# Eighty-eight fixed elementwise operations become the scheduler's choice between VectorE and GpSimd, with changed cost formulas and a newly searched schedule

## The chip, the cores and the metric

The kernel runs as one program on one core of a Trainium2 chip. The metric is the device time of one execution in microseconds (us); before and after are compared as medians of several executions. A profile is one further execution, recorded by the hardware. Its engines are called PE (TensorE's matmuls), PEld (TensorE's weight loads), DVE (VectorE), ACT (ScalarE), POOL (GpSimd) and SP (SyncE, which issues transfers).

## The reference

A four-layer decoder over x (8 batches of 256 tokens, 256 features) with a context of 77 tokens per batch. Each layer is an attention, a cross attention and a feed-forward part, each with a residual sum and a layer norm after it; most parts are of another kind in every layer. Two parts matter here. The cross attention of layer 2 normalises its queries per head (16 features) and rotates pairs of them:

```
q = _layernorm(q, qn_w, qn_b)
qp = q.reshape(b, h, s, d // 2, 2)
qe, qo = (qp[..., 0], qp[..., 1])
out = jnp.stack([qe * cos - qo * sin, qe * sin + qo * cos], axis=-1)
```

Layer 3 begins with a state-space block, whose output is gated, and goes on with a linear cross attention, whose queries and keys pass a softmax over the 16 features of each head:

```
y = _rmsnorm(y * jax.nn.silu(z), norm_w)
...
q = jax.nn.softmax(_heads(x @ Wq.T + bq), axis=-1)
k = jax.nn.softmax(_heads(y @ Wk.T + bk), axis=-1)
```

The other parts (quantised attention in layer 0, mixtures of experts, attention with learned features, a butterfly feed-forward) are computed as before.

## The kernel before

Tokens are in 16 tiles of 128; a batch is two tiles, a block four. Nearly all matrix products are float32, with tiles of 128x128 (or 32, 64 or 77 rows or columns for heads), accumulating in eight PSUM banks. Every layer runs its parts batch by batch, and generators interleave parts that don't depend on each other: in layer 3 the state-space block of one batch (`inputs`, `weights`, `outputs`) runs beside the cross attention (`cross`) and the feed-forward part (`dense`) of earlier ones.

The order in which each engine works is not the program's own. The class `Arrange` builds the program once, turns it into a graph of some 20,900 instructions and schedules it by a list scheduler, engine by engine, with a cost in ns for each instruction (`cost`: how long it holds its engine, and when its result is there), for matmuls that follow each other (`pair`), for signals between engines (`SIGNAL`) and for two states of TensorE's clock. The program is then built again with that order tied in (`chain`). A stretch of 100 instructions is scheduled with one of eight pairs of slack factors; the string `CHOICE` has one digit per stretch, found by a search outside of the kernel. So each change of a cost or a digit can move instructions anywhere behind it.

Some operations may run on either of two engines: `either` records both forms, and the scheduler takes the one that it can start first. Before the change these are copies from PSUM (`copy`, L612 on DVE and L613 on ACT), copies with a bias or a scale (L619, L620, L626), the first tap of the convolution (L2655 or L2656) and the differences in `weights` of layer 3 (L2697 or L2700).

The operations that the change frees are, with their fixed engines before:

- L2 cross attention, `rotated`, per batch: two strided products u (L2304, POOL), q times own (L2308, DVE), plus more (L2309, DVE), and their sum into qpad (L2310, POOL). The result is transposed by PE (L779). The rotation of batch b+2 is issued while batch b is weighed.
- L3 `outputs`, the gate: after each pair of L2747 (DVE) one product y times zs (L2752, POOL); ACT squares it (L2756), POOL sums the squares (L2757), and PE adds them over partitions.
- L3 `head_softmax`, for queries (q, 128x512) and for keys (kv, 77x256): maximum (L2933), subtraction (L2934, DVE), exponential (L2935, ACT), sum and reciprocal (L2937, L2938, DVE), and the division as a product (L2939, POOL). PE takes kv as weights (L633) and transposes q (L2801).

Lines that the text also speaks of: the norms are bn_stats (L730), POOL's scale and power for the inverse root (L660, L661) and the application (L741; in layer 3, in place, L2782), which PE transposes next (L713; L2843). POOL's sums of x and a row are L753, L2796 and L2854. L2661 are the other taps of the convolution, L2863 the Gelu of `dense`. L1713 belongs to the routing of layer 0's experts, and L2246 are memsets that prepare layer 2's cross attention.

## Time and profile before

| what | value |
|---|---|
| median of three runs | 3106.22 us (3105.67 to 3116.44) |
| the profiled execution | 3120.3 us, span 3118.6 us |
| mean granted TensorE clock | 0.944 |
| PE, DVE, ACT, POOL busy | 2951.5, 1666.5, 1217.5, 932.5 us |
| PE busy in the first 468 us | 395.9 us |
| PE busy from 2184 to 2418 us (L2 cross attention) | 219.3 us |
| PE busy from 2652 to 3120 us (most of L3) | 422.5 us |
| activation table loads on ACT | 58, 1.283 us each |

The page gives busy time per engine, then the span in 40 slices of 78 us: each digit is the busy share in tenths, and PEclk the granted clock in tenths of full speed. A row of the windows view gives a stretch, its length, then busy us and the number of instructions of PE, PEld, DVE, ACT and POOL, then the granted clock, the share of transfers and GB/s. A row of the waits view gives who waited, for whom, us in total, how often, and the longest. The view of one line gives its instructions with minimum, median and maximum duration in ns; the timeline gives start, duration, engine and line.

### The profile page before, as it was taken

The page shows a single profiled execution, that of the slowest core. Times are in us where ns is not written, and L with a number is a line of the kernel's source. Part 1 is how long each engine was busy: PE and PEld are TensorE (multiplying, and loading weights), DVE is VectorE, ACT ScalarE, POOL GpSimd, SP SyncE. Part 2 cuts the span into 40 slices and gives each one's busy share as a digit, 9 for nine tenths or more (in the row PEclk, how much of TensorE's full clock was granted, in tenths as well). Part 3 has the DMA queues.
Part 4 walks back from the last instruction along what each step waited for, and adds up shares of the span by engine and source line. Part 5 has one row for each costly group of instructions (what it writes and reads, how often), then busy time and mean ns, then how long its engine had stood idle before and what let it go on. Part 6 is the DMA issues. An engine that isn't in the chain of part 4 may idle for free. (4 is left out here: it accounts for less than half of the span.)

```text
span 3118.6 us, 49555 instructions
## 1 busy us (share of the span) xinstructions
PE 2951.5 (95%) x19200; PEld 2162.8 (69%) x19200; DVE 1666.5 (53%) x4467; ACT 1217.5 (39%) x2725; POOL 932.5 (30%) x1413
## 2 busy tenths in 40 slices
PE   6899979989998999999999999999899999999997
PEld 4456557768886777776555777566577687677876
DVE  7878776660003666775112221366677542678872
ACT  4667544433332334443111111255344233355442
POOL 2222353353323221332000000322244463535342
PEclk7879879999998999999999999999888999989998
DMA  5424550125542000011010243300000564100000
GB/s 188 137 94 160 202 193 27 33 88 201 195 175 97 18 8 10 28 61 54 11 56 1 97 145 122 98 28 8 1 15 32 186 242 157 32 11 4 8 8 11
DMA packets 136364, 252.87 MB, mean 81 GB/s; under 512 B 14962, under 2 KB 104826, under 8 KB 128442
## 3 DMA queue, kind: packets, MB, share of 16 engines
q1 hardware_dynamic: 112298, 150.80, 14.5%
q0 software_dynamic: 22672, 97.77, 9.0%
q8 instruction: 155, 2.54, 0.3%
q10 hardware_dynamic: 1152, 1.05, 0.1%
q14 instruction: 87, 0.71, 0.1%
HBM read 162.32 MB, written 87.26 MB: 80 GB/s over the span
## 5 line engine op out<-in xcount | busy, mean ns | idle before, releaser
L633 PE MATMUL ps<-xt,w 128*128 128x256 f32 (+1 forms) x1408 | 443.6, 462 | 4.9 <-issue 4.3
L633 PE MATMUL ps<-w,hT 128*128 128x256 f32 (+1 forms) x1704 | 378.7, 379 | 0.0
L633 PEld LDWEIGHTS ps<-xt,w 128*128 128x128 f32 x1408 | 260.8, 192 | 148.0 <-issue 124.3
L633 PEld LDWEIGHTS ps<-w,hT 128*128 128x128 f32 (+1 forms) x1704 | 313.2, 186 | 53.5 <-issue 5.2
L633 PE MATMUL ps<-gT,w 128*128 128x256 f32 (+2 forms) x1472 | 337.1, 386 | 1.0 <-ACT gT L613 0.7
L633 PEld LDWEIGHTS ps<-gT,w 128*128 128x128 f32 x1472 | 263.1, 190 | 67.7 <-ACT hT L1662 2.9
L633 PE MATMUL ps<-w,oT 128*128 128x256 f32 x704 | 162.0, 382 | 0.0
L753 POOL TENSOR_TENSOR xb<-x,rows 128x256 f32<-128x256 f32 x80 | 59.2, 743 | 301.6 <-DVE res L758 294.5
L633 PEld LDWEIGHTS ps<-w,oT 128*128 128x128 f32 x704 | 131.7, 190 | 22.3 <-issue 2.5
L613 ACT COPY y<-ps 128x512 f32<-128x512 f32 (+2 forms) x65 | 31.0, 476 | 251.9 <-PE ps L633 243.2
L1735 ACT ACTIVATE hT<-ps 128x512 f32<-128x512 f32 x56 | 33.4, 597 | 233.7 <-PE ps L633 233.7
L1160 ACT ACTIVATE e<-ps,nm 128x128 bf16<-128x128 f32 (+1 forms) x256 | 103.5, 441 | 38.3 <-DVE nm L1155 30.9
L1739 DVE TENSOR_TENSOR hT<-hT,ps 128x512 f32<-128x512 f32 x56 | 38.5, 687 | 146.7 <-PE ps L633 146.5
L612 DVE COPY gT<-ps 128x256 f32<-128x256 f32 (+1 forms) x12 | 4.6, 391 | 209.1 <-PE ps L1607 170.8
L613 ACT COPY oT<-ps 128x256 f32<-128x256 f32 (+1 forms) x130 | 58.2, 448 | 112.6 <-PE ps L1882 55.5
L2093 DVE SCALAR_TENSOR_TENSOR f<-ps,f 128x512 f32<-128x512 f32 x128 | 79.2, 682 | 30.3 <-ACT f L2092 30.2
L1984 DVE TENSOR_TENSOR hT<-hT,ps 128x320 f32<-128x320 f32 x64 | 31.2, 487 | 117.2 <-PE ps L633 117.2
L1662 ACT ACTIVATE hT<-ps,more 128x256 f32<-128x256 f32 (+1 forms) x152 | 70.1, 462 | 55.8 <-PE ps L633 55.3
L613 ACT COPY xt<-ps 128x256 f32<-128x256 f32 (+2 forms) x105 | 44.3, 432 | 116.8 <-PE ps L713 92.1
L2092 ACT ACTIVATE f<-ps,neg 128x512 f32<-128x512 f32 x128 | 77.5, 693 | 30.2 <-PE ps L2089 30.1
L1400 ACT ACTIVATE P<-P 128x616 f32<-128x616 f32 (+1 forms) x48 | 42.6, 888 | 115.3 <-DVE P L1439 114.9
L661 POOL TENSOR_TENSOR rs<-rs,mhalf 128x1 f32<-128x1 f32 x144 | 80.5, 563 | 9.4
(675 smaller groups left out, 6507.8 us busy)
## 6 DMA issues: line engine op xcount, KB each, us to landing
l2x<-zero SPq DMA_DIRECT2D x28, 1024.0 KB
l0x<-zero SPq DMA_DIRECT2D x16, 1024.0 KB
w<-in_L_ffn_rg SPq DMA_DIRECT2D x8, 1024.0 KB
w<-in_L_ffn_ru SPq DMA_DIRECT2D x8, 1024.0 KB
w<-in_L_ffn_rd SPq DMA_DIRECT2D x8, 1024.0 KB
l0e<-y SPq DMA_DIRECT2D x17, 256.0 KB
l2e<-y SPq DMA_DIRECT2D x15, 256.0 KB
rows<-in_rows SPq DMA_DIRECT2D x7, 544.0 KB
```

Source lines behind the costliest of these rows:

```text
L613: ("Activation", ("InstTensorCopy", None), lambda: nc.scalar.copy(out, in_)),
L633: self.nc.tensor.matmul(out, lhsT, rhs, start=(i == 0), stop=(i == last))
L661: self.nc.gpsimd.tensor_tensor(out, out, self.mhalf[: in_.shape[0], :w], ALU.pow)
L753: self.nc.gpsimd.tensor_tensor(t, self.X[i], row, ALU.add)
L1160: nc.scalar.activation(e[:, : (t + 1) * P], ps[j][:, i, :], AF.Exp, bias=nm[:, t, h : h + 1], accum_out=z[:, t, h : h + 1],)
L1400: nc.scalar.activation(pr, pr, AF.Exp, scale=0.125)
L1662: nc.scalar.activation(hT[:, f + m, :w], ps[:, m * 256 : m * 256 + w], func, bias=more[:, f + m : f + m + 1])
L1735: nc.scalar.activation(hT[:, f, :], ps, func, **({"bias": bias(f)} if bias else {}))
L1739: nc.vector.tensor_tensor(hT[:, f, :], hT[:, f, :], ps, ALU.mult)
L1984: nc.vector.tensor_tensor(hT[:, f, :CAP], hT[:, f, :CAP], ps[:, :CAP], ALU.mult)
L2092: nc.scalar.activation(f[:, j], ps[j], AF.Exp, bias=neg1)
L2093: nc.vector.scalar_tensor_tensor(f[:, j], ps[j], 1.0, f[:, j], ALU.max, ALU.min)
```

## The change

A helper `product` makes an operation of two SBUF tiles free between DVE and POOL, and the operations above go through it. At the same time five formulas in `cost` change: float32 matmuls, DVE operations with a pointer scalar and two SBUF tiles, ACT's copies, ACT's activations with an accumulated sum, and ACT's activations of 500 to 600 elements. The string `CHOICE` is another one (209 digits, of which 53 differ, the first of them the sixth). So the order changes on every engine from layer 0 on.

```diff
-            own = n / 2.4 * (1 if not wide or turn else 4) + 3
+            own = n / 2.4 * (1 if not wide or turn else 4) + (9 if wide and not turn else 3)
...
             s = 65 + n / 0.96
+            pairs = sum(self.count(x.ap) > 200 for x in ins) > 1
             if n <= 256 and ps and kind == "InstTensorScalarPtr" or kind == "InstCopyPredicated":
                 s += 60
+            elif kind == "InstTensorScalarPtr" and pairs and not ps:
+                s += 72
...
             if kind == "InstTensorCopy":
-                s = 23 + 0.9 * n
-                return s, s + 115
-            s = 144 + 0.83 * n + (108 if last else 0) + (45 if not ps and 64 < n <= 512 else 0)
+                s = 118 + 0.746 * n
+                return s, s + 110
+            s = 144 + 0.83 * n + ((87 if n < 200 else 46) if last else 0) + (45 if not ps and 64 < n <= 512 else 0)
+            if 500 < n < 600:
+                s -= 50
...
+    def product(self, out, a, b, op=ALU.mult):
+        nc = self.nc
+        self.either(*(
+            (w, ("InstTensorTensor", None), lambda e=e: e.tensor_tensor(out, a, b, op))
+            for w, e in (("DVE", nc.vector), ("Pool", nc.gpsimd))
+        ))
+
...
                 for u in range(2):
-                    nc.gpsimd.tensor_tensor(
-                        u2[:, :, :, u::2], q[:, :, :, 1 - u :: 2], over(other[:, :, :, u]), ALU.mult
-                    )
+                    self.product(u2[:, :, :, u::2], q[:, :, :, 1 - u :: 2], over(other[:, :, :, u]))
                 flat = lambda t: t.rearrange("p t d u -> p t (d u)")
-                nc.vector.tensor_tensor(u1, q, over(flat(own)), ALU.mult)
-                nc.vector.tensor_tensor(u1, u1, over(flat(more)), ALU.add)
-                nc.gpsimd.tensor_tensor(qp, u1, u2, ALU.add)
+                self.product(u1, q, over(flat(own)))
+                self.product(u1, u1, over(flat(more)), ALU.add)
+                self.product(qp, u1, u2, ALU.add)
...
-                        nc.gpsimd.tensor_tensor(y[:, h, :], y[:, h, :], zs[:, h, :], ALU.mult)
+                        self.product(y[:, h, :], y[:, h, :], zs[:, h, :])
...
-        nc.vector.tensor_tensor(q, q, bc(m), ALU.subtract)
+        self.product(q, q, bc(m), ALU.subtract)
...
-        nc.gpsimd.tensor_tensor(q, q, bc(z), ALU.mult)
+        self.product(q, q, bc(z))
```

More of the change, by code (lines that the diff above doesn't have):

```diff
@@ L78 @@
     PART, TRIALS = 100, ((1.0, 1.0), (0.5, 0.5), (2.0, 2.0), (2.0, 0.5), (0.5, 2.0), (0.25, 0.25), (4.0, 1.0), (1.0, 4.0))
-    CHOICE = "21111100022110201121001101001100121011210222022111000101101010101012110000000022022202222222222222211111001010010100010000000010010110100110100201010100221121012111111101111000120011111011000121111010011010111"
+    CHOICE = "21111002120111001121021011220111111111011102122111000101101010101010112000000001022212222122222222211101001010010101010000000010111010100110121201010110220001010121111111111000100010100111111101011010010011111"
     def __init__(self, g):
```

## The prediction

> **What bounds the kernel now.** First the page: the busy row, the slices and the granted clock.

> ```profile
> PE 2951.5 (95%) x19200; PEld 2162.8 (69%) x19200; DVE 1666.5 (53%) x4467; ACT 1217.5 (39%) x2725; POOL 932.5 (30%) x1413
> ...
> PE   6899979989998999999999999999899999999997
> ...
> PEclk7879879999998999999999999999888999989998
> ```

> TensorE is busy 95% of the span of 3118.6 us: only some 167 us are open, and they lie at the two ends (slices 1 to 6 and 29 to 40). The clock falls in the same places. Its mean is 0.944. Cut into windows, the trace shows stretches at 0.50 (2228.5 to 2252 us) and at 1.00, so about 2 x 0.056 x 3118.6 = 349 us run at half speed. That costs up to half of them, 175 us: as much as the idle time. Then the windows in which the rescheduled products lie, L2's cross attention (the first row) and L3 (the others), with columns PE, PEld, DVE, ACT, POOL, clock:

> ```profile
> 2262.00:2340.00 78.00, 76.57 (x708) 54.67 (x706) 60.42 (x216) 33.74 (x76) 32.24 (x45) 0.89 0.04 15
> 2808.00:2886.00 78.00, 70.30 (x415) 57.45 (x414) 63.78 (x152) 44.27 (x80) 38.14 (x53) 0.96 0.01 4
> 2886.00:2964.00 78.00, 74.89 (x445) 63.87 (x444) 63.80 (x160) 38.31 (x70) 30.98 (x49) 1.00 0.02 8
> 3042.00:3120.00 78.00, 57.55 (x253) 47.39 (x251) 22.45 (x68) 16.92 (x33) 14.62 (x32) 0.86 0.03 11
> ```

> DVE is the fullest helper there (64 of 78 us), GpSimd has room. Last TensorE's own waits, from 2652 to 3042 and (last line) from 3042 us on:

> ```profile
> PE ps L2843 <- DVE x L2782: 5.8, 5, 1.8
> ...
> PE ps L633 <- POOL kv L2939: 2.9, 1, 2.9
> ...
> PE ps L633 <- POOL zs L2757: 0.8, 1, 0.8
> PE ps L2801 <- POOL q L2939: 0.6, 1, 0.6
> ```
> ```profile
> PE ps L2843 <- DVE x L2782: 7.6, 3, 3.8
> ```

> So the products themselves end few waits. What TensorE waits for most is the normalisation x of L2782, on DVE.

> **The change part by part.** Durations of the moved products (minimum/median/maximum ns, by line):

> ```profile
> L2752 POOL TENSOR_TENSOR w<-w,zs x16: 1262/1270/1319, 2772.6 to 3033.7; 128x512 f32<-128x512 f32 x16
> ```
> ```profile
> L2939 POOL TENSOR_TENSOR kv<-kv,hv x8: 616/630/1108, 2663.7 to 2739.3; 77x256 f32<-77x256 f32 x8
> L2939 POOL TENSOR_TENSOR q<-q,hv x8: 1057/1062/2591, 2810.1 to 3064.9; 128x512 f32<-128x512 f32 x8
> ```
> ```profile
> L2934 DVE TENSOR_TENSOR kv<-kv,hm x8: 357/414/541, 2660.3 to 2736.3; 77x256 f32<-77x256 f32 x8
> L2934 DVE TENSOR_TENSOR q<-q,hm x8: 684/1078/1436, 2807.0 to 3061.1; 128x512 f32<-128x512 f32 x8
> ```

> *Where they go.* The order of the changed program puts on DVE 14 of the 16 gate products (L2752), all 8 q and all 8 kv divisions (L2939), and on GpSimd one q and one kv subtraction (L2934). In L3 GpSimd loses 14 x 1.27 + 8 x 1.06 + 8 x 0.63 = 31.3 us and gains, at its own division rows, 1.06 + 0.63: 29.6 us less. DVE gains 22 x 0.69 + 8 x 0.41 - 1.1 = 17.4 us. The planner also moves five copies (0.43 us) and nine of L2655/L2697 (0.48 us) off DVE to ScalarE: 6.5 us. Net +11 us on DVE. In L2's rotation 5 of 16 u products and 2 of 8 last sums go to DVE, 3 of 8 q-own products and 6 of 8 sums to GpSimd: at 0.84 and 1.27 us on GpSimd, 0.42 (the 128x256 rows) and 0.69 on DVE, that is 2.7 us off DVE and some 4 us onto GpSimd. Both are hidden: the rotation of batch b+2 runs while batch b is weighed, and GpSimd is busy 32 of 78 us. Uncovered they would cost those 4 us.

> *What gets shorter.* (a) The 2.9 us wait for kv: its reciprocal ended at 2662.31, but GpSimd was at a power, a copy and a memset and began the product at 2663.70. On DVE, where the reciprocal stands, it would end near 2662.8 instead of 2664.35: -1.5 us; behind that the matmuls wait for nothing else in the row. (b) q ready earlier: -0.6. (c) The gate pair 2 x (1.27 - 0.69) = 1.2 earlier: -0.8 for zs. (d) L2782 is held by GpSimd:

> ```profile
> 3032.43 2.54 POOL L2752 TENSOR_TENSOR w<-w,zs 128x512 f32<-128x512 f32 x2
> ...
> 3032.70 1.14 DVE L2782 TENSOR_SCALAR x<-x,mv,rs 128x256 f32<-128x256 f32 x1
> ```

> It takes 1.14 us instead of 0.41 and ends 0.15 us behind the first product; TensorE then waits 1.01 us for it. In the changed order 16 matmul records stand between the two transposes that wait here: -1.0. At 3064.44 the second x is held likewise by a q division; now that division (0.69) stands ahead of it on DVE instead: -0.2. (e) The first rotation (TensorE waits 0.8 us for qpad): its u pair took 2.60 us on GpSimd; now each engine takes one: -0.8. Sum of (a) to (e): -4.9 us.

> *What is added.* No wait on another engine: the products now follow their makers on DVE. Behind them queue the norms (bn_stats, L2782). ACT gets five more table loads in L2's shared part and L3, 5 x 1.283 = 6.4 us (58 to 63 in all), chiefly Gelu, exp and Gelu again within a batch. ACT is under 60% busy there, so TensorE's work on the next batch hides it. Bounds of both: 0 if all is hidden, 11 + 6.4 = 17.4 if all lands on the path. I take +2, nearest to the rows that show room.

> *What is only reordered.* TensorE's tile shape changes go from 965 to 946 (39 fewer ahead of L2's expert block, 20 more behind it). A 128x256 float32 matmul starts 0.216 us after its like and 0.309 us where the next shape is 77*64: 0.093 x 19 = -1.8. In L2's two attentions six copies leave DVE (2.6 us) with the 2.7 above, beside a DVE busy 171 of 234 us at a reduced clock: I take -2, of 0 to -5.3. The new search touches L0 most, where orders move farthest. No row prices that: its bounds are the 72 us that TensorE idles in the first 468 us on one side and as much added on the other; the rows nearest to it are the three runs of one order, which spread by 10.8 us. Are the corrected costs nearer to the trace? float32 128x256 pairs start 432 ns apart (the planner said 430, now 436), ScalarE's 128x512 activations 476 (569, now 519), DVE's two-tile L2661 396 (332, now 404), but ScalarE's 128x256 copies about 268 at the tightest (253, now 309). Mostly yes: -3.

> *The sum.* -4.9 + 2 - 1.8 - 2 - 3 = -9.7, say -10 us. The profiled execution took 3120.3 us (span 3118.6, 1.7 around it), so by its rows 3110. It is 14 us above the median of 3106.2; carried over, the forecast is **3096 us** (-0.3%).

> *A rule to weigh.* The rows show DVE held until a GpSimd operation ends, also in two-input products: q's L2934 takes up to 1.436 us against 0.684. [...]

> **The rivals.**
> 1. *The clock decides (faster).* If the shorter stalls spare a tenth of the 175 us lost at half speed, the time is 3106 - 10 - 17 = 3079. For it: the low-clock stretches lie where the change acts and where the order moves most. Against: the largest stalls (11 us before L1713, 4.35 us of DVE behind the memsets of L2246) stay in the new order. [...]
> 2. *DVE becomes L3's bound (slower).* Place: x L2782 and its statistics queue behind products that GpSimd used to take. It decides once the 11 us and the loads no longer fit into DVE's 14 us of idle time per window. Then all 17.4 us are on the path and the gains are lost: 3106 + 17 = 3123. For it: DVE at 82%, L2782 is TensorE's largest wait. Against: GpSimd's holds on DVE shrink by 30 us.
> 3. *Nothing ends on it.* The waits move to L2782 and the search trades one stall for another: 3106.

> **How the numbers follow.** What a measurement tells from no change is about 0.5%, 15.5 us: 3090.7 and 3121.8. Forecast 0.30, rival 3 0.18: same 0.48. Rival 1: 0.31. Rival 2: 0.17, and 0.04 for an order of L0 that is worse by as much: slower 0.21. The range runs from past rival 1 (a further half of its 17 us) to rival 2: 3070 to 3125.

> **What would show it.** GpSimd's busy time 25 to 30 us lower (about 905), DVE's about 5 higher; no wait of TensorE on L2939; L2782's waits below 13.4 us; 63 table loads. Wrong, if L2782's waits grow past 20 us (rival 2), if the mean clock leaves 0.944 by over 0.01 (rival 1 or its reverse), or if the first 468 us change by more than all of L3.

## The result, and the profile after

The changed kernel took 3107.61 us (median of 12 executions, 3103.66 to 3111.57), the kernel before, beside it on the same chip (A below), 3116.43 us (12 executions, 3105.67 to 3124.49). The ratio is 0.9971, with a 95% interval of 0.996 to 0.9982: 0.3% faster, 8.8 us. On three other chips the same pair gave 0.9985 (0.997 to 1.0001), 0.9961 (0.9948 to 0.9975) and 0.998 (0.9964 to 0.9995).

The forecast of 3096 us stood on the median of the three executions shown, 3106.22; twelve give one 10.2 us higher, and two of those three are the lowest of the twelve. Against the twelve, 3096 us is a fall of 20.4 us, more than twice the 8.8 measured. The effect itself was forecast at -10 us: near in size, but the steps that make it up are not those that the stages show.

The profiled execution of the changed kernel, 3111.57 us, is the slowest of its twelve. Its page, in the rows that the prediction showed of before:

```profile
PE 2949.0 (95%) x19200; PEld 2164.8 (70%) x19200; DVE 1663.8 (54%) x4474; ACT 1231.8 (40%) x2749; POOL 899.0 (29%) x1387
...
PE   6889979989999999999999999999899999999997
...
PEclk7788979999999999999999999999888999999998
```

The span is 3109.9 us, the mean clock 0.946. GpSimd is 33.5 us less busy, TensorE hardly changed. Behind line 630 the changed kernel's lines are 10 to 12 higher (L2782 is now L2792, L633 is L645); every product is on the helper's line, L631. In its source view the products stand where the order had put them:

```profile
L631 DVE TENSOR_TENSOR w<-w,zs x14: 679/691/1262, 2771.8 to 3025.8; 128x512 f32<-128x512 f32 x14
...
L631 DVE TENSOR_TENSOR kv<-kv,hv x8: 407/420/434, 2662.8 to 2734.6; 77x256 f32<-77x256 f32 x8
L631 DVE TENSOR_TENSOR q<-q,hv x8: 687/692/694, 2799.6 to 3055.7; 128x512 f32<-128x512 f32 x8
```

The durations are those that the forecast used (0.69, 0.42, 0.69). TensorE's waits of the changed kernel in layer 3, from 2629 us to the end:

```profile
PE ps L2853 <- DVE x L2792: 11.2, 9, 3.8
PE ps L645 <- DVE w L2979: 4.0, 2, 2.3
```

The waits for x fell from 13.4 to 11.2 us, and none on a product of the keys is left (2.9 before). That on the queries' division fell from 0.6 to 0.2 us, and that for w rose from 3.2 to 4.0. Now the two parts in which the products lie, cut at TensorE's last matmul of each part: layer 2's cross attention, then all of layer 3 (columns as before: stretch, length, PE, PEld, DVE, ACT, POOL, clock). Before:

```profile
2217.70:2407.30 189.60, 178.17 (x1539) 129.07 (x1539) 140.79 (x484) 71.37 (x159) 83.06 (x127) 0.84 0.04 17
2625.20:3118.60 493.40, 445.09 (x2273) 351.99 (x2272) 330.31 (x848) 219.40 (x387) 196.28 (x310) 0.93 0.07 21
```

After:

```profile
2208.50:2411.20 202.70, 188.93 (x1541) 139.04 (x1541) 138.04 (x480) 71.39 (x160) 86.71 (x129) 0.78 0.04 16
2628.90:3109.90 481.00, 439.47 (x2272) 346.17 (x2272) 332.72 (x862) 232.07 (x406) 169.22 (x282) 0.95 0.07 21
```

Layer 3 is 12.4 us shorter: TensorE's idle time fell from 48.3 to 41.5 us (length less PE), its busy time by 5.6 us for the same matmuls, and the clock rose. Layer 2's cross attention is 13.1 us longer at about equal idle time (11.4 and 13.8 us): there the clock fell from 0.84 to 0.78. The rest comes from ahead of it, which ends 9.2 us earlier.

### The profile page after: what moved, and what is told of

It reads as the page before. It is cut to its first block, busy times and chain, and to the rows that moved or that the text cites. A ratio compares the mean times of both kernels' runs of the same rounds, so it can differ in the third digit from the quotient of the medians.

```text
span 3109.9 us, 49528 instructions
## 1 busy us (share of the span) xinstructions
PE 2949.0 (95%) x19200; PEld 2164.8 (70%) x19200; DVE 1663.8 (54%) x4474; ACT 1231.8 (40%) x2749; POOL 899.0 (29%) x1387
## 3 DMA queue, kind: packets, MB, share of 16 engines
q1 hardware_dynamic: 112298, 150.80, 14.6%
q8 instruction: 155, 2.54, 0.3%
## 5 line engine op out<-in xcount | busy, mean ns | idle before, releaser
L645 PE MATMUL ps<-xt,w 128*128 128x256 f32 (+1 forms) x1408 | 442.1, 461 | 0.1
L645 PE MATMUL ps<-w,hT 128*128 128x256 f32 (+1 forms) x1704 | 378.7, 379 | 0.0
L645 PEld LDWEIGHTS ps<-xt,w 128*128 128x128 f32 x1408 | 259.2, 191 | 142.7 <-issue 121.2
L645 PEld LDWEIGHTS ps<-w,hT 128*128 128x128 f32 (+1 forms) x1704 | 313.1, 186 | 53.5 <-issue 4.7
L645 PE MATMUL ps<-gT,w 128*128 128x256 f32 (+2 forms) x1472 | 336.6, 386 | 0.9 <-ACT gT L618 0.7
L645 PEld LDWEIGHTS ps<-gT,w 128*128 128x128 f32 x1472 | 263.2, 190 | 66.9 <-ACT hT L1674 2.3
L645 PE MATMUL ps<-w,oT 128*128 128x256 f32 x704 | 162.4, 384 | 0.0
L645 PEld LDWEIGHTS ps<-w,oT 128*128 128x128 f32 x704 | 132.8, 191 | 21.9 <-issue 1.8
L1412 ACT ACTIVATE P<-P 128x616 f32<-128x616 f32 (+1 forms) x48 | 42.6, 888 | 120.3 <-DVE P L1451 119.8
```

What stands on the lines that cost most here:

```text
L645: self.nc.tensor.matmul(out, lhsT, rhs, start=(i == 0), stop=(i == last))
L1412: nc.scalar.activation(pr, pr, AF.Exp, scale=0.125)
```

## How the runs are read

Every execution lists its span and mean clock. In the clock records of the profiles before and after, the granted clock is 1.00 or 0.50 and nothing between. Span times clock is what the execution would take at full speed, and the rest is lost to half clock (an estimate: a wait that falls into half clock counts only half). The means, with the chip of each set of runs (the kernel before takes 3175.6 us on chip B and 3165.2 on C, 3118.4 on D and 3118.8 on E, so only neighbours are compared; each row has 12 executions, but 8 in e4 and e5, 6 in e11, and 29 to 35 of the kernel before):

| chip | kernel | ratio to before (95%) | mean span | full-speed part | lost to clock |
|---|---|---|---|---|---|
| B | before | | 3172.7 | 2977.3 | 195.4 |
| B | e1: free products, old order | 1.0007 (0.9986-1.0027) | 3176.4 | 2978.1 | 198.3 |
| B | e2: new order, tied products | 1.0002 (0.998-1.0024) | 3175.2 | 2978.8 | 196.4 |
| B | e3: rotation tied | 1.0039 (1.0016-1.0062) | 3184.5 | 2985.5 | 199.0 |
| B | e4: old digits in L2 | 0.9931 (0.9907-0.9955) | 3156.1 | 2976.2 | 179.9 |
| C | before | | 3164.0 | 2972.7 | 191.3 |
| C | e5: before again | 1.0022 (1.0004-1.004) | 3167.9 | 2971.9 | 196.0 |
| C | e6: after again | 0.9985 (0.997-1.0001) | 3160.6 | 2971.7 | 188.9 |
| C | e7: alternating | 0.9988 (0.9973-1.0003) | 3158.7 | 2976.2 | 182.5 |
| C | e8: clumped | 0.9975 (0.996-0.9989) | 3157.0 | 2969.7 | 187.3 |
| D | before | | 3117.4 | 2946.8 | 170.6 |
| D | e9: after | 0.9961 (0.9948-0.9975) | 3106.4 | 2946.9 | 159.5 |
| D | e10: new order, tied products | 0.9998 (0.9981-1.0015) | 3117.3 | 2949.7 | 167.6 |
| D | e11: old digits in L2 | 0.9948 (0.9931-0.9965) | 3103.8 | 2948.1 | 155.7 |
| D | e12: L3's products tied | 0.9977 (0.9961-0.9992) | 3110.5 | 2947.9 | 162.6 |
| E | before | | 3116.9 | 2947.9 | 169.0 |
| E | e13: new from L2's cross attention on | 0.9979 (0.9966-0.9992) | 3109.1 | 2946.4 | 162.7 |
| E | e14: new ahead of it | 1.0028 (1.0013-1.0043) | 3123.9 | 2950.0 | 173.9 |
| E | e15: after | 0.998 (0.9964-0.9995) | 3109.3 | 2949.7 | 159.6 |
| E | e16: before again | 1.0008 (0.9991-1.0025) | 3118.9 | 2947.8 | 171.1 |

Chip D shows it most plainly: the changed kernel is 11.0 us faster, its full-speed part is the same to 0.1 us, and the 11.1 us are all clock. On E the full-speed part even grows by 1.8 and the clock gives 9.4. The difference of two full-speed parts has a standard error of 1.2 to 1.7 us (2.0 and 2.2 for e5 and e16), so 5 us less of waits at full speed would show.

The profiles give the stages ("half" is the time at clock 0.50 in the trace's clock records). Each is one execution, and they are unequal draws: after (A) is the slowest of its twelve, e9 and e15 are the fastest of theirs.

| profile (chip) | up to L2's attention end | L2 cross attention (half) | L2 experts | L3 (half) |
|---|---|---|---|---|
| before (A) | 2217.7 | 189.7 (61.4) | 217.9 | 493.4 (71.0) |
| e16: before (E) | 2219.0 | 184.2 (51.2) | 217.7 | 495.6 (74.2) |
| after (A) | 2208.5 | 202.7 (88.7) | 217.7 | 481.0 (50.3) |
| e9: after (D) | 2206.9 | 194.3 (64.9) | 216.9 | 480.2 (47.0) |
| e15: after (E) | 2209.7 | 193.2 (64.9) | 217.6 | 481.0 (47.0) |
| e10: tied products (D) | 2212.0 | 199.7 (71.7) | 219.4 | 482.3 (46.9) |
| e12: L3 tied (D) | 2211.1 | 202.7 (88.7) | 217.6 | 484.5 (50.4) |
| e13: back new (E) | 2216.8 | 187.0 (61.4) | 217.1 | 480.7 (50.2) |
| e14: front new (E) | 2212.2 | 201.3 (81.9) | 218.4 | 492.2 (67.5) |

## The experiments

**Theory after the result (A):** the gain is clock. The new order takes half-clock time out of layer 3 and puts some into layer 2's cross attention, where long rows of head matmuls lower the clock. **Rivals:** (B) the freed products bring the gain by shorter waits, as steps (a) to (e) said; (C) the new order brings it and the products are idle ballast.

**Products alone, order alone, and parts.** e1 is the changed kernel with the old costs and digits:

```diff
-            own = n / 2.4 * (1 if not wide or turn else 4) + (9 if wide and not turn else 3)
+            own = n / 2.4 * (1 if not wide or turn else 4) + 3
```

and so on for the other formulas and `CHOICE`. e2 is the changed kernel with each product tied to its engine of before; e3 ties only the four products of the rotation:

```diff
-    def product(self, out, a, b, op=ALU.mult):
+    def product(self, out, a, b, op=ALU.mult, on=("DVE", "Pool")):
...
-            for w, e in (("DVE", nc.vector), ("Pool", nc.gpsimd))
+            for w, e in (("DVE", nc.vector), ("Pool", nc.gpsimd)) if w in on
...
-                self.product(u1, q, over(flat(own)))
+                self.product(u1, q, over(flat(own)), on=("DVE",))
```

e4 gives the changed kernel before's digits for layer 2's cross attention (the stretches 153 to 169: 21121012111111101 instead of 20001010121111111).

> The kernel before with the products freed and nothing else: the old cost formulas and the old digits. (A) If the freedom itself is worth the -4.9 us that the prediction summed for it, the ratio to before is near 0.998. (B) If what counts is the order that a search fitted to the graph, an unfitted order loses: 1.000 to 1.004, most of it in the attention of layer 0 and the cross attention of layer 2.

> The changed kernel with every product tied to its engine of before; the new cost formulas and digits stay. (A) Products: the gain in layer 3 goes, ratio 0.999 to 1.000. (B) Order: most of the gain stays, 0.997 to 0.998, and the cross attention of layer 2 is as slow as in the changed kernel (216 us between its marks instead of 204), since its shape changes on TensorE are 75 against 74 there and 86 before.

> The changed kernel with layer 2's rotation tied to its engines of before, layer 3 free. (A) If GpSimd's longer products of the rotation cost the 13 us that layer 2's cross attention lost, these come back: ratio about 0.993. (B) If the order does (fewer alternations of head matmuls and whole tiles, so more time at half clock), the stage stays at 212 us or more: 0.997.

> The changed kernel with the digits of before in the 17 stretches of layer 2's cross attention alone. (A) If the new digits there are what is bad, its 13 us come back: 0.993. (B) If it is the amount of alternation, which this kernel does not restore (74 shape changes in the stage, in longer runs than in either kernel), the stage stays at 212 us or more: 0.997 or above.

Measured: 1.0007, 1.0002, 1.0039, 0.9931. Neither the products nor the order alone gains anything, and with layer 3's products free but the rotation tied it is slower (its full-speed part grows by 8.2 us; where is open). That speaks against (B) and (C) alike: the two seem worth something only together. Two limits: the changed kernel itself did not run on this chip, and the digits of e1 and e2 were searched for programs with the products elsewhere, so neither has an order fitted to it. e4 was the fastest kernel, as (A) of its expectation said, but its profile doesn't show the reason given there: its cross attention took 206.7 us at a clock of 0.78.

**Controls, and the theory of the head matmuls.** In layer 2's cross attention TensorE's tile shape changes 97 times before and 84 after, by the traces of the stage as cut above (86 and 74 by the count that the expectations use), so head matmuls stand in longer rows. e7 and e8 change only the 17 digits of that part, to 27706212121751111 (114 changes in the trace, 103 by that count) and 14041410156111311 (77 and 67). e5 and e6 are the two kernels unchanged.

> The kernel before, unchanged: its stages on the chip of the comparison, and what equal programs differ by. Ratio 1.000 with no theory against it; a cross attention of layer 2 near 61 us at half clock if that belongs to the order, as in the first profile, or near 100 us if it belongs to the chip, as in the four kernels before.

> The changed kernel, unchanged, beside the others. Ratio 0.996 to 0.998 if its gain is one of the order that any chip shows; 1.000 or above if the gain hangs on where a chip's clock windows fall, since its relative with the rotation fixed was 1.004.

> The changed kernel with other digits in the 17 stretches of layer 2's cross attention, chosen for alternation: 103 shape changes of TensorE in that stage instead of 74, head matmuls in runs of 15 on the mean instead of 20. (A) If long runs of head matmuls are what drops the clock, the stage spends 20 us or more less at half clock than in the next kernel and is 10 us shorter. (B) If each shape change costs 0.093 us and the clock does not care, it is 3 us longer than the changed kernel.

> As the kernel before it, but with digits chosen for few changes: 67 in the stage, runs of 22. (A) Clock: at least as much half clock as the changed kernel, and 10 us longer than the alternating one. (B) Shape changes: 3 us shorter than the alternating one.

Measured: e5 1.0022, with an interval that leaves out 1 for a program compared with itself. So a difference of 0.2% between two sets of runs proves nothing by itself. e6 0.9985. In the profiles e7's stage took 194.4 us with 58.0 at half clock, e8's 202.9 with 85.3, e6's 208.3 with 99.0, as the theory has it. But the medians of e7 and e8 (0.9988, 0.9975) don't follow, and e9 and e15, with the changed kernel's own order, later showed 64.9 at half clock where A had shown 88.7. One profile of that stage is one draw: the theory of the head matmuls is not shown, and falls as an explanation of the result.

**The same four cells on one chip.** e9 is the changed kernel, e10 is e2 again, e11 is e4 again, and e12 ties only layer 3's products (the gate and the division to POOL, the subtraction to DVE).

> The changed kernel unchanged, as the yardstick for the three kernels beside it on the same chip. Ratios to the kernel before so far were 0.9971 on one chip and 0.9985 on another: a gain that is real and small gives 0.995 to 1.000 here; a result above 1.002 would say that the gain belongs to one chip.

> The changed kernel's costs and search, with all products tied to the engines that they had before. If the freed products bring the gain (steps a to e of the forecast, 4.9 us), it is some 5 us (0.16%) slower than the changed kernel beside it. If the new order alone brings it, and the products' engines end on no path, the two are equal within 0.2% (6 us), as L3's last stage of 368.7 us with tied products against 371.3 with free ones suggests.

> The changed kernel with the digits that the kernel before had for L2's cross attention; this gave 0.9931 once, on a chip on which the changed kernel itself did not run. If L2's order in the changed kernel loses by the clock what the profiles show (27 us more at half clock, 13 us), this is 0.2 to 0.4% faster than the changed kernel beside it. If the 0.9931 was scatter, the two agree within 0.2%.

> The changed kernel with only L3's products (gate, subtraction, division) tied to their engines of before; L2's rotation stays free. If freeing L3's products is worth the forecast's steps a to d (4.1 us), L3's last two stages (480.9 and 481.8 us with free products) are some 4 us longer here and a wait of TensorE on a product of keys or queries returns. If the order alone removed those waits, the stages stay within 2 us.

Measured: 0.9961, 0.9998, 0.9948, 0.9977. From e10 to e12 (rotation freed) the mean span falls by 6.8 us, from e12 to e9 (layer 3's products freed) by 4.1; with 12 runs and standard deviations of 5.6 to 7.4 us these two carry an error of some 2.5 us each, and e5 gave 3.9 us by the same measure for nothing; only their sum, 10.9 us or 0.35%, stands well clear of that. Of it 2.8 us are full-speed part and 8.1 clock. The order of every engine up to the cross attention is the same in all three kernels, so these 10.9 us should come from behind it. The profiles don't show where: from its begin to the end e10 takes 1101.4 us, as long as the changed kernel on A, against 1091.4 and 1091.8 in e9 and e15. e11 and e9 are alike within 0.2%: the version with the old digits is the fastest twice over, but not shown faster than the changed kernel. The rows of layer 3, products tied (e10):

```profile
2631.10:3113.40 482.30, 435.70 (x2273) 344.79 (x2272) 325.09 (x841) 229.68 (x399) 195.50 (x310) 0.95 0.07 21
```

Tied, TensorE idles 46.6 us there, against 41.5 to 42.6 with free products (after, e9, e15) and 48.3 before. So the freed products do shorten the waits, by some 4.5 us. The largest of them shows it best, that for x, in e10:

```profile
PE ps L2853 <- DVE x L2792: 13.7, 11, 3.8
```

In all eighteen profiles of this case these waits sum to 13.4 to 13.7 us where layer 3's products are tied (seven profiles) and to 9.6 to 11.6 us where they are free (eleven), with old and new orders on both sides. The wait for kv is another matter: e2, e10, e12 and e14 lack it too, with the division still on GpSimd. In e10 TensorE multiplies without a gap from 2661.6 us until the product for kv has ended at 2667.8. The waits for zs and for q's division are not in e10's list either. So the wait on a product of keys or queries that e12's expectation looked for did not return, though its layer 3 is some 4 us longer as expected (484.5 against 480.2 to 481.0).

But e10's length is 482.3 against 480.2 to 481.0, because TensorE's busy time is 2 to 4 us longer in those three, at about the same half-clock time; why is open. What makes layer 3 11 us shorter than before is there without the products: the clock row says 0.95 against 0.93.

**Front or back.** The costs and the digits can be exchanged in mid-plan, at stretch 153, the begin of layer 2's cross attention:

```diff
         for i in range(0, len(self.nodes), self.PART):
+            if i // self.PART == self.AT:
+                self.again()
```

where `again` prices all instructions that are not yet placed by the other formulas. e13 has old costs and digits ahead of that point and the new ones with free products behind; e14 the reverse, with tied products.

> TensorE's order up to layer 2's cross attention is that of the kernel before; from there on the new costs, the new digits and the free products plan (on a different state, so the order behind is near the changed kernel's, not equal to it). If the gain comes from the products and the new order behind 2206 us, this has it nearly whole: 0.996 to 0.998. If it comes from the front (the three profiles of the changed kernel on chips of this speed reach that point 9 to 11 us earlier than the one of before), this stays at 0.999 to 1.002.

> The reverse: TensorE's order up to layer 2's cross attention is the changed kernel's; behind it the old costs, the old digits, and all products on their engines of before. If the gain comes from the front, 0.996 to 0.998. If it comes from behind 2206 us, 0.999 to 1.002, as the kernel with the new search and tied products gave (1.0002 and 0.9998).

> The changed kernel unchanged, as the yardstick on this chip: 0.996 to 0.9985 by the three results so far.

> The kernel before unchanged, as a second control: 0.998 to 1.002. It also gives one more profile of before, to see how far its stages scatter.

Measured: 0.9979, 1.0028, 0.998, 1.0008. The part behind, alone, has the whole gain; the part ahead, alone, has none. In its profile e14 does reach the cross attention early (2212.2 against 2219.0) and loses it at once, in a cross attention of 201.3 us. That loss does not go with the cross attention's own digits, costs or products: e14 has those of before there and 81.9 us at half clock, e13 the new ones and 61.4, as much as the first profile of before. In the nine profiles of the table it goes with the order ahead, 51.2 to 61.4 us behind the old one and 64.9 to 88.7 behind the new. But on C e7, with the new order ahead, had 58.0, and on B e1, with the old one, ran that part at a clock of 0.76. So the cause is open. The two unchanged kernels on chip E, before (e16):

```profile
2219.00:2403.20 184.20, 172.73 (x1539) 127.15 (x1539) 141.20 (x484) 71.65 (x159) 83.03 (x127) 0.86 0.05 17
2620.90:3116.50 495.60, 447.92 (x2272) 355.20 (x2272) 331.03 (x848) 219.70 (x387) 196.40 (x310) 0.93 0.06 21
```

and after (e15):

```profile
2209.70:2402.90 193.20, 179.07 (x1541) 131.64 (x1541) 138.79 (x480) 71.34 (x160) 86.70 (x129) 0.83 0.04 16
2620.50:3101.50 481.00, 438.41 (x2273) 345.75 (x2272) 333.54 (x862) 232.22 (x406) 168.66 (x282) 0.95 0.07 21
```

They repeat chip A in kind: -9.3 us ahead, +9.0 in the cross attention, -14.6 in layer 3. (The two executions lie 15.0 us apart, the medians of the changed kernel and the kernel before on this chip 8.7.) Of the last, 5.1 us are idle time and 9.5 busy time of the same matmuls.

## Where layer 3's clock comes from

Layer 3 has the half-clock time in pieces of 3.41 us or multiples (but for the last, which runs on past the program's end: 8.13 us before, 7.97 after): 11 stretches in the profile of before and 13 in e16, but 7 in after, 6 in e15 and, with tied products, 8 in e10. In each execution their beginnings stand on one grid of 3.413 us, whose offset differs between executions (2.96, 1.03, 1.22 and 3.00 us in these four). Nearly every stretch follows a wait of TensorE: in the 3.413 us ahead of it TensorE was busy for at most 66% in all 11 cases of before and at most 58% in all 7 of after. One wait shows it in rows, that for x of L2782 with 1.83 us. In e16 it begins at 2861.85 us; the three rows are cut on the grid:

```profile
2861.37:2864.79 3.42, 1.58 (x9) 0.78 (x8) 2.98 (x10) 0.02 (x1) 3.00 (x6) 1.00 0.02 5
2864.79:2868.20 3.41, 3.41 (x20) 3.38 (x20) 3.34 (x7) 2.10 (x3) 2.60 (x5) 0.50 0.00 0
2868.20:2871.61 3.41, 3.41 (x24) 2.25 (x28) 1.57 (x4) 1.67 (x2) 0.00 (x0) 0.50 0.00 0
```

TensorE was busy 1.58 of 3.42 us (46%), and the next two windows ran at 0.50 though it was busy throughout. In the first profile of before the same wait, as long, begins at 2868.51 us and lies across a line of that grid:

```profile
2863.31:2866.72 3.41, 3.41 (x18) 2.95 (x17) 3.41 (x8) 1.95 (x3) 2.22 (x4) 1.00 0.11 38
2866.72:2870.13 3.41, 1.79 (x11) 1.28 (x9) 2.97 (x11) 1.33 (x4) 1.68 (x4) 1.00 0.11 38
2870.13:2873.55 3.42, 2.88 (x20) 2.24 (x20) 3.42 (x8) 1.48 (x2) 2.71 (x5) 1.00 0.00 0
```

The window that holds most of it is busy for 1.79 us (52%), and the clock stays. So one wait of 1.83 us costs 1.83 us in one execution and, as an estimate from these rows, 1.83 + 6.83/2 = 5.2 us in the next. In six profiles (before, e16, after, e9, e13, e15) every such window of layer 3 at full speed that was busy for less than 46% was followed by half clock (6 of 6 in before, 4 of 4 in after). Between 46 and 58% both happened (2 of 7 and 3 of 5). In the four with the new order none above 58% was; in the two of before six were, at 60 to 95%, for which no reason is shown.

So single waits that the new order took away can have cost more than their length. Before, the two waits of 0.91 and 1.01 us for L2782 at 3031.5 and 3032.9 us (step (d) of the forecast) are followed by 3.41 us at half clock, in both profiles; in the changed order one of 0.91 us is left, and no half clock follows. But e10, with tied products, lacks that stretch too: the order, not the product's engine, removes it.

## Why the prediction was right or wrong

- **The total** (-10 us; measured -8.8, a ratio of 0.9967 forecast and 0.9971 measured) was right in size, and that was luck, since its steps were not what gave it. The absolute time was 11.6 us too low, 10.2 of it by the base: the step that carried the sum over to the median of three executions. By the rows of the profiled execution the sum gave 3110, 2.4 us too high.
- **(a) to (d), -4.1 us of waits in layer 3:** right as waits, but for the larger part not by the products' engine. The wait for kv is gone (a), that for q fell from 0.6 to 0.2 (b), the one for zs from 0.8 to 0.3 (c). All three are gone with tied products as well (e10), so the order removes these 2.9 us (1.5 + 0.6 + 0.8) of the forecast. L2792's waits are 2.2 us lower (d, 1.2 forecast), and that is the products' doing. The wait for kv had cost more than its 2.9 us: in the profile of before 10.24 us at half clock begin at 2665.33 us, just behind it (in the window from 2661.92 us on TensorE was busy for 27%), and 6.8 us in two pieces near it in e16, against 3.4 in after and e13 and none in e9 and e15. Freed products cut TensorE's idle time in layer 3 by some 4.5 us (46.6 to about 42). As time they are worth less in the profiles, 1 to 4 us (e10 and e12 against e9), since TensorE's busy time grows by up to 4.
- **(e), -0.8 us:** TensorE's wait for qpad is gone, and it is back (0.8) in e10. By its own prices the forecast should have had 4.7 us more on GpSimd there, not some 4. The rotation's freedom may be worth more in runs, 6.8 us with an error of 2.5. No step had that, since the rotation was costed as hidden behind the weighing of earlier batches, and no profile shows it: e10's cross attention of 199.7 us lies within the 193.2 to 202.7 of the kernels with a free rotation and the same order ahead.
- **Added +2:** no run prices it by itself. DVE's busy time in layer 3 grew by 2.4 us where the forecast had 11: operations that stay on DVE became shorter (the subtraction for q 0.69 us at the median, 1.08 before, but 0.69 in e10, too). That GpSimd holds them less is not shown to be the reason. GpSimd's time in layer 3 fell by 27.1 us (29.6 forecast), and the table loads are 63, as counted.
- **Tile shape changes, -1.8, and layer 2's attentions, -2:** the second is wrong in sign; the first is not seen alone in any run. The cross attention grew by 13.1 us on A and 9.0 on E. Half of its added half-clock time (27.3 and 13.7 us) accounts for all of it on A and 6.9 us on E; TensorE's idle time grew by 2.4 and 2.6.
- **The search in layer 0, -3:** right in size, but as clock. The 3589 matmuls that ended within the first 468 us of before end at 464.1 in the changed kernel, and at 465.8 against 469.5 on chip E, with 23.9 and 13.7 us less at half clock, which more than accounts for it. The whole part ahead of the cross attention ends 7 us earlier on chips A, D and E (2216.8 to 2219.0 in three profiles of the old order, 2206.9 to 2213.3 in seven of the new), and 0 to 8 us later on B and C (2246.4 and 2247.4 against 2247.0 to 2254.8). The cross attention takes it back (e14).
- **The step that failed**, beside the base, is a missing term: the forecast had no clock in its sum. It put that into rival 1, 17 us more for a tenth of the half-clock loss. Half-clock loss did fall, by 11.1 of 170.6 us on D (6.5%), but in place of the waits' gain and not on top of it: the full-speed part is unchanged. Rival 1's mechanism, half-clock time spared, was the true one there, with a net price of 9.4 us (E) to 11.1 us (D) in place of 17 on top.
- **Rivals 2 and 3:** DVE did not become the bound (L2792's waits fell). Something did end on the change, but not for the products alone or the order alone (e1, e2, e10), where rival 3 is what was measured.
- **DVE held until a GpSimd operation ends** (the prediction's 1.436 us against 0.684): in the profile of before the long L2934 ran from 2922.95 to 2924.39 us beside GpSimd's L2757, which ended at 2923.84, 0.55 us ahead of it, and the short one, from 2999.88 us, had no GpSimd operation beside it. That products on DVE hold GpSimd's powers in turn is not shown. Those on two and four columns do take longer in layer 3 (the eight on two 727 ns before, 979 after), first before, then after:

```profile
L661 POOL TENSOR_TENSOR r<-r,mhalf 128x2 f32<-128x2 f32 (+1 forms) x12 | 9.9, 827 | 1.0
```
```profile
L673 POOL TENSOR_TENSOR r<-r,mhalf 128x2 f32<-128x2 f32 (+1 forms) x12 | 12.0, 996 | 0.9
```

  But with tied products (e10) they take 938 ns, so most of that goes with the new order and only 0.7 us with the products on DVE; the many powers on one column went from 573 to 584 ns. L2792's waits fell all the same, from 13.4 to 11.2 us.
- **What would show it:** GpSimd 899.0 (905 forecast), DVE 2.7 lower instead of 5 higher, a wait of 0.2 us on the division (L2939) left, L2792's waits below 13.4, 63 loads; the first 468 us changed by less than layer 3 (3.9 against 12.4). The mark for the clock, 0.01 off 0.944, was too coarse: it is 31 us of time, and rival 1's own 17 us would have moved the mean by 0.0055. The means of the runs on D are 0.9453 before and 0.9487 after, a change of 0.0034 that carries the whole gain.

**Open** are why the changed kernel loses clock in layer 2's cross attention, where the 10.9 us between tied and free products lie, why TensorE's busy time in layer 3 grows with free products, and why the front gains on three chips and not on two. On C its first 3589 matmuls still end 1.5 us earlier (464.8 in e6, 466.3 in e5) and the loss comes behind them.

## What to carry to other kernels

## What the runs showed of the hardware

- The same program takes 3116 to 3119 us on three chips and 3165 and 3176 on two others, at mean clocks of 0.945 to 0.946 (D and E) and 0.938 to 0.940. Its full-speed part is longer there, too (2973 and 2977 against 2947 us), in the parts between layer 0's attention and layer 2's cross attention (e5 takes 11 and 19 us more than the first profile of before in its two stretches) and in layer 2's experts (10 us); this is the kernel before, unchanged. Why is open.
- A program against itself gave 1.0022 (1.0004 to 1.004) and 1.0008 (0.9991 to 1.0025): single ratios within 0.2% of each other say nothing here.
- In e16 a window of 3.413 us in which TensorE was busy for 46% (1.58 of 3.42 us, from 2861.37 us on) was followed by two at 0.50; in before, one at 52% (1.79 of 3.41 us, from 2866.72 us on) by none. The same order shows 64.9 (e9, e15) or 88.7 us (after) of half clock in one stage of some 200 us, layer 2's cross attention.
- With layer 3's products free to run on DVE, TensorE's waits for x there sum to 9.6 to 11.6 us, with tied ones to 13.4 to 13.7, in all eighteen profiles.
